# A selective scan on one core: 11 of every 32 readout multiplications moved from VectorE to GpSimd, and the accumulation on TensorE put one unit later

## The chip, the core and the metric

The kernel runs on one core of a Trainium2 chip. A core has five engines that run their own instruction queues in order and wait for each other through semaphores: TensorE (PE; its weight loads are PEld), VectorE (DVE), ScalarE (ACT), GpSimd (POOL) and SyncE (SP, which here only issues DMAs). SBUF and PSUM are the two on-chip memories; both have 128 partitions. The metric is the device time of one execution in microseconds, lower is better. The kernel before takes 8464.05 us, the median of five runs (8449.98 to 8479.84).

## The reference, cut to what matters

The whole computation is a two-layer network on an image batch of 2 x 128 x 64 x 64. Layer 0 is a deformable convolution block and a mixture of experts; layer 1 is a state-space block (a selective scan) and a second mixture of experts. The change touches only the scan of layer 1:

```
delta = softplus(delta + dt_proj_b)
A = -exp(A_log)
dA  = exp(delta * A)             # for each of 256 channels, 16 states n, 4096 positions l
dBu = delta * B[n, l] * x
s[l] = dA[l] * s[l-1] + dBu[l]
y[l] = sum over n of s[l, n] * C[n, l]
y = (y + x * D) * silu(z)
out = out_proj_w @ y
```

So for each channel, state and image there is a first-order recurrence over 4096 positions, and its states are multiplied with C and summed over the 16 states.

## The kernel before, in words

**Pieces and units.** The positions of an image are cut into 8 pieces of 512 (`LC`), so two images make 16 pieces. In a piece the 16 states and the 2 halves of the channels make 32 *units*; a unit is one tile of 128 channels x 512 positions. The loop of `scan` (from L1286 on) goes through all 512 units. The program keeps the order in which instructions are written (`manual_schedule`), so the order of every queue is the order of this loop.

**One unit u.** VectorE runs the recurrence as one scan instruction (L1301). It reads the decay `da` from PSUM and the input `db` from SBUF and writes the states back over `da` in PSUM. Then VectorE multiplies the states with C (`bc[:, 1, :]`), which gives `sc` in SBUF (L1311; the pool has 5 buffers of it). TensorE transposes the four 128-column blocks of `sc` with an identity and adds them up in a PSUM tile `py` (`add`, L1271); these additions stand at the end of the loop's body and take the `sc` of the unit before. ScalarE copies the last column of the states to `state` for the next piece (`keep`, L1308, one unit later).

**What is made ahead.** `drive` (L1246) lets GpSimd multiply `du` with B into `db`, three units ahead (`AHEAD`), with four buffers, so `db` of unit u+3 can only be written when the scan of unit u-1 is done. `decay` (L1253) lets ScalarE compute `da` two units ahead, in three PSUM buffers, so `da` of unit u+2 can only be written when unit u-1 has been read. `fetch` has SyncE broadcast rows of B and C (`bcb`).

**The side work.** While a piece is scanned, the next one is prepared by a generator (`prepare`), two steps a unit: 12 GpSimd multiplications and additions of 128x512 (L1151 x4, L1156 x2, L1166 x2, L1185 x2, L1213 x2), and on VectorE L1159 x2, L1195, L1197, L1204 x3, L1206 and L1209. `project` closes the piece before with three more (L1347 x2, L1362). While the first image is scanned, a second generator (`rest`) runs five steps a unit: the end of layer 0 and the convolutions of layer 1 for the second image, on TensorE, ScalarE, VectorE and by DMA.

Of the kernel before, what the change touches and what calls it, by code (L numbers as in the profile page):

```python
# [9 lines left out]
F32 = mybir.dt.float32  # L10
I32 = mybir.dt.int32
AF = mybir.ActivationFunctionType
ALU = mybir.AluOpType
# [5 lines left out]
P = 128  # L19
# [20 lines left out]
DS = 16  # L40
LC = 512
# [793 lines left out]
TB = 1  # L835
AHEAD = 3
BCB = 6


def view(ap, offset, dims):  # L840
# [28 lines left out]
class L1Conv:  # L869
# [351 lines left out]
    def scan(self, sp, ps, pp, rest):  # L1221


        env, nc = self.env, self.env.nc
        states = [sp.tile([P, 2, DS], F32, name=f"state{b}", bufs=1) for b in range(B)]
        for state in states:
            nc.vector.memset(state, 0.0)
        NK = N // LC

        def nxt(k):  # L1230

            res = {}
            return self.prepare(k // NK, k % NK, sp, pp, res), res

        gen, res = nxt(0)
        for _ in gen:
            pass
        units = [(k, n, half) for k in range(B * NK) for n in range(DS) for half in range(2)]
        pieces, das, dbs, bcb, tail = {0: res}, {}, {}, {}, iter(())

        def drive(u):

            if u < len(units):
                k, n, half = units[u]
                dbs[u] = sp.tile([P, LC], F32, name="db", bufs=AHEAD + 1)
                nc.gpsimd.tensor_tensor(dbs[u], pieces[k]["du"][:, half, :], bcb[u // 2][:, 0, :], ALU.mult)  # L1246

        def decay(u):
            if u < len(units):
                k, n, half = units[u]  # L1250
                das[u] = ps.tile([P, LC], F32, name="da", bufs=3)
                dl = pieces[k]["dl"][:, half, :]
                nc.scalar.activation(das[u], dl, AF.Exp, scale=self.A[:, half, n : n + 1])  # L1253

        def fetch(i):
            for i in range(len(bcb), i + 1):
                k, n = divmod(i, DS)
                if "bc" not in pieces.get(k, {}):
                    break
                bcb[i] = sp.tile([P, 2, LC], F32, name="bcb", bufs=BCB)  # L1260
                nc.sync.dma_start(out=bcb[i], in_=pieces[k]["bc"][n].partition_broadcast(P))

        adds, py = deque(), []

        def add(half, what, first, last):

            if first:
                py.append(ps.tile([P, GT, P], F32, name=f"py{half}", tag=f"py{half}", bufs=1))
            out = py[half]
            for j in range(GT):  # L1270
                nc.tensor.matmul(  # L1271
                    out[:, j, :],
                    what[:, j * P : (j + 1) * P],
                    env.ident,
                    is_transpose=True,
                    start=first and j == 0,
                    stop=last and j == GT - 1,
                )

        fetch(BCB - 3)  # L1280
        for u in range(AHEAD):
            drive(u)
        decay(0)
        decay(1)
        side, keep = Side(), None
        for u, (k, n, half) in enumerate(units):  # L1286
            now, i, state = pieces[k], u // 2, states[k // NK]
            if n == 0 and half == 0:
                side.add(tail)
            last = n == DS - 2 and half == 0  # L1290
            if last and k == NK - 1:
                rest.drain()

            if k + 1 < B * NK and k + 1 not in pieces and (k != NK - 1 or not rest.todo):
                gen, pieces[k + 1] = nxt(k + 1)
                side.add(gen)
            fetch(i + BCB - 2)
            bc = bcb[i]

            s = das.pop(u)  # L1300
            nc.vector.tensor_tensor_scan(s, s, dbs.pop(u), state[:, half, n : n + 1], ALU.mult, ALU.add)  # L1301
            if last:
                side.drain()
                fetch(i + BCB - 2)
            drive(u + AHEAD)

            if keep:
                nc.scalar.copy(*keep)  # L1308
            decay(u + 2)
            sc = sp.tile([P, LC], F32, name="sc", bufs=5)  # L1310
            nc.vector.tensor_tensor(sc, s, bc[:, 1, :], ALU.mult)  # L1311
            keep = state[:, half, n : n + 1], s[:, LC - 1 : LC]
            for _ in range(2 if rest.todo or k != NK - 1 else 4):
                side.step()
            for _ in range(5):
                rest.step()

            while adds:
                add(*adds.popleft())
            if n == 0 and half == 0:  # L1320
                py.clear()
                adds.extend((h, now["dx"][:, h, :], True, False) for h in range(2))
            adds.append((half, sc, False, n == DS - 1))
            if n == DS - 1 and half == 1:
                add(*adds.popleft())
                yt = sp.tile([P, 2, GT, P], F32, name="yt", bufs=1)
                tail = self.project(k // NK, k % NK, tuple(py), yt, now["zz"], now["xr"], pp)
        for _ in tail:
            pass
# [311 lines left out]
```

## Time and profile before

One execution was profiled. It took 8480.65 us, 0.8 us above the slowest of the five runs; its span from the first to the last instruction of the program is 8478.9 us, so 1.75 us lie outside.

| stretch of the span, us | length, us | what runs |
|---|---|---|
| 0 to 6101.7 | 6101.7 | layer 0, and layer 1's convolutions of the first image |
| 6101.7 to 7473.2 | 1371.5 | scan of the first image (units 0 to 255) beside the rest of the second image's earlier stages |
| 7473.2 to 8027.0 | 553.8 | scan of the second image, pieces 8 to 14 (units 256 to 479) |
| 8027.0 to 8093.8 | 66.8 | the last piece (units 480 to 511); nothing more is prepared |
| 8093.8 to 8478.9 | 385.1 | the second mixture of experts |

Over the span VectorE is busy 5712.4 us (67%), GpSimd 4588.7 us (54%), ScalarE 2127.9 us (25%) and TensorE 5962.2 us (70%). In the page's rows, `out<-in` names the tiles that an instruction writes and reads; then come the number of instructions, the busy time, the mean duration in ns and, after a bar, the idle time of the engine just ahead of these instructions with what ended it. In the list of waits, a line says who waited for whom, the sum in us, the number of times and the longest one. A bare number pair at the head of a timeline row is the start and the duration in us.

### The profile page before, as it was taken

The page shows a single profiled execution, that of the slowest core. Times are in us where ns is not written, and L with a number is a line of the kernel's source. Part 1 is how long each engine was busy: PE and PEld are TensorE (multiplying, and loading weights), DVE is VectorE, ACT ScalarE, POOL GpSimd, SP SyncE. Part 2 cuts the span into 40 slices and gives each one's busy share as a digit, 9 for nine tenths or more (in the row PEclk, how much of TensorE's full clock was granted, in tenths as well). Part 3 has the DMA queues.
Part 4 walks back from the last instruction along what each step waited for, and adds up shares of the span by engine and source line. Part 5 has one row for each costly group of instructions (what it writes and reads, how often), then busy time and mean ns, then how long its engine had stood idle before and what let it go on. Part 6 is the DMA issues. An engine that isn't in the chain of part 4 may idle for free. (4 is left out here: it accounts for less than half of the span.)

```text
span 8478.9 us, 85143 instructions
## 1 busy us (share of the span) xinstructions
PE 5962.2 (70%) x28533; PEld 4203.4 (50%) x28533; DVE 5712.4 (67%) x8472; ACT 2127.9 (25%) x4442; POOL 4588.7 (54%) x4556
## 2 busy tenths in 40 slices
PE   2678888888888857667666676667556566755569
PEld 2456666666666635344434343444344455533359
DVE  1577777777777767777886658666557735599940
ACT  1111111111111114111112121212353444555520
POOL 0456666666666666665665656666534323367600
PEclk7789999999989979878888878888766655656555
DMA  4677666666666678777777777776553334334323
GB/s 125 183 245 216 196 206 213 194 214 193 208 212 194 213 221 274 250 227 220 222 233 201 218 210 223 216 214 199 168 178 112 114 89 121 110 120 136 126 89 124
DMA packets 658558, 1574.35 MB, mean 186 GB/s; under 512 B 168164, under 2 KB 280588, under 8 KB 645580
## 3 DMA queue, kind: packets, MB, share of 16 engines
q0 software_dynamic: 307200, 1006.88, 39.8%
q1 hardware_dynamic: 287980, 494.19, 18.5%
q10 hardware_dynamic: 62944, 67.83, 2.3%
q8 instruction: 232, 3.80, 0.2%
q14 instruction: 202, 1.65, 0.1%
HBM read 1450.99 MB, written 120.01 MB: 185 GB/s over the span
## 5 line engine op out<-in xcount | busy, mean ns | idle before, releaser
L547 POOL DMA_INDIRECT v<-table,idx x3840 | 3649.7, 950 | 2394.8 <-issue 995.4
L597 PE MATMUL out<-st,regw 128*128 128x512 f32 x3840 | 2120.0, 677 | 164.5 <-issue 110.0
L558 DVE TENSOR_TENSOR v<-v,pw 128x1024 f32<-128x1024 f32 x960 | 1168.8, 1218 | 1075.4 <-DMA v<-table,idx 917.1
L568 PE MATMUL pst<-ident,v 128*128 128x128 f32 x7680 | 1243.5, 305 | 800.1 <-issue 482.6
L577 ACT COPY st<-pst 128x512 f32<-128x512 f32 x960 | 558.6, 586 | 4345.9 <-remote 2485.3
L568 PEld LDWEIGHTS pst<-ident,v 128*128 128x128 f32 x7680 | 1008.0, 157 | 1142.5 <-issue 755.5
L564 DVE TENSOR_TENSOR v<-v,low 128x512 f32<-128x512 f32 x1920 | 1318.2, 687 | 65.6
L563 DVE TENSOR_TENSOR low<-v,pw 128x512 f32<-128x512 f32 x1920 | 1329.3, 692 | 33.4
L1246 POOL TENSOR_TENSOR db<-du,bcb 128x512 f32<-128x512 f32 x512 | 660.6, 1295 | 956.6 <-DVE da L1301 909.5
L597 PEld LDWEIGHTS out<-st,regw 128*128 128x128 f32 x3840 | 763.3, 221 | 770.6 <-issue 707.6
L334 PEld LDWEIGHTS po<-wout,ring 128*128 128x128 f32 x5120 | 743.2, 199 | 369.5 <-issue 367.7
L334 PE MATMUL po<-wout,ring 128*128 128x147 f32 x5120 | 798.7, 300 | 162.8 <-issue 158.0
L1301 DVE TENSOR_TENSOR_SCAN da<-da,state,db 128x512 f32<-128x512 f32 x512 | 657.1, 1283 | 292.9 <-ACT da L1253 274.6
L1271 PE MATMUL py<-ident,sc 128*128 128x128 f32 x2048 | 466.8, 381 | 333.6 <-DVE sc L1311 333.0
L1271 PEld LDWEIGHTS py<-ident,sc 128*128 128x128 f32 x2048 | 341.9, 198 | 475.6 <-DVE sc L1311 436.5
L1311 DVE TENSOR_TENSOR sc<-da,bcb 128x512 f32<-128x512 f32 x512 | 354.1, 692 | 48.6 <-DVE da L1301 1.9
L1253 ACT ACTIVATE da<-delta,w_A_log 128x512 f32<-128x512 f32 x512 | 354.0, 692 | 17.3 <-DVE delta L1209 1.5
L972 PE MATMUL ps<-tm,X 120*88 120x48 f32 x2048 | 254.9, 304 | 75.8 <-ACT Y L924 36.7
L972 PEld LDWEIGHTS ps<-tm,X 120*88 120x88 f32 x2048 | 250.3, 219 | 107.9 <-ACT Y L924 49.3
L959 PE MATMUL ps<-ident,hs 64*120 64x64 f32 x1408 | 142.8, 271 | 136.5 <-ACT X L924 87.9
L959 PEld LDWEIGHTS ps<-ident,hs 64*120 64x120 f32 x1408 | 125.7, 177 | 197.6 <-ACT X L924 105.6
L988 PE MATMUL ps<-ident,Y 88*64 88x88 f32 x768 | 109.1, 294 | 144.7 <-ACT img L924 86.6
(268 smaller groups left out, 5090.8 us busy)
## 6 DMA issues: line engine op xcount, KB each, us to landing
bcb<-bc SPq DMA_DIRECT2D x256, 512.0 KB
regw<-in_regw SPq DMA_DIRECT2D x66, 1280.0 KB
v<-table,idx POOLq DMA_INDIRECT x3840
yd<-ys ACTq DMA_DIRECT2D x128, 256.0 KB
yc<-yd SPq DMA_DIRECT2D x32, 1024.0 KB
gb<-gd SPq DMA_DIRECT2D x16, 2048.0 KB
tm<-pos SPq DMA_DIRECT2D x16, 1440.0 KB
table<-xn SPq DMA_DIRECT2D x128, 128.0 KB
```

The source lines that it names most:

```text
L334: m()
L547: nc.gpsimd.indirect_dma_start(out=v[:, j, :], out_offset=None, in_=self.table[b], in_offset=bass.IndirectOffsetOnAxis(ap=idx[:, j, t : t ...
L558: nc.vector.tensor_tensor(up, up, w, ALU.mult)
L563: nc.vector.tensor_tensor(low, v4[:, two, 2:4, :], w, ALU.mult)
L564: nc.vector.tensor_tensor(up[:, two], up[:, two], low, ALU.add)
L568: nc.tensor.matmul(pt[:, j, :], v4[:, j, q, :], env.ident, is_transpose=True, start=j == 0 and q == 0, stop=j == GT - 1 and q == 1,)
L577: nc.scalar.copy(st, pt.rearrange("p j t -> p (j t)"))
L597: nc.tensor.matmul(self.out[half], self.regw[t // CH][:, t % CH, half * P : (half + 1) * P], st, start=first, stop=last,)
L972: nc.tensor.matmul(ps[:, c, :], X[:, c0 + c, :], tm[:, :, c0 + c], start=True, stop=True)
L1246: nc.gpsimd.tensor_tensor(dbs[u], pieces[k]["du"][:, half, :], bcb[u // 2][:, 0, :], ALU.mult)
L1271: nc.tensor.matmul(out[:, j, :], what[:, j * P : (j + 1) * P], env.ident, is_transpose=True, start=first and j == 0, stop=last and j == GT ...
L1301: nc.vector.tensor_tensor_scan(s, s, dbs.pop(u), state[:, half, n : n + 1], ALU.mult, ALU.add)
```

## The change

In units 2, 5, 7, 10, 13, 15, 18, 21, 23, 26 and 28 of each piece the scan writes its states to the `sc` tile in SBUF instead of over `da` in PSUM, and the multiplication with C is done by GpSimd, in place, in the unit after, behind that unit's `db` on GpSimd's queue. In the other 21 units nothing moves on VectorE. For all units, the additions on TensorE come two units behind instead of one; what is left is added at the end of the piece. No buffer is added. In the changed kernel `db` is written at L1247, the scan stands at L1305, the new GpSimd multiplication at L1316 and the one left on VectorE at L1321.

```diff
+ASIDE = (2, 5, 7, 10, 13, 15, 18, 21, 23, 26, 28)
...
-        side, keep = Side(), None
+        side, keep, lag = Side(), None, None
...
             s = das.pop(u)
-            nc.vector.tensor_tensor_scan(s, s, dbs.pop(u), state[:, half, n : n + 1], ALU.mult, ALU.add)
+            aside = u % (2 * DS) in ASIDE
+            sc = sp.tile([P, LC], F32, name="sc", bufs=5)
+            to = sc if aside else s
+            nc.vector.tensor_tensor_scan(to, s, dbs.pop(u), state[:, half, n : n + 1], ALU.mult, ALU.add)
...
             decay(u + 2)
-            sc = sp.tile([P, LC], F32, name="sc", bufs=5)
-            nc.vector.tensor_tensor(sc, s, bc[:, 1, :], ALU.mult)
-            keep = state[:, half, n : n + 1], s[:, LC - 1 : LC]
+
+            if lag:
+                nc.gpsimd.tensor_tensor(*lag, ALU.mult)
+                lag = None
+            if aside:
+                lag = sc, sc, bc[:, 1, :]
+            else:
+                nc.vector.tensor_tensor(sc, s, bc[:, 1, :], ALU.mult)
+            keep = state[:, half, n : n + 1], to[:, LC - 1 : LC]
...
-            while adds:
-                add(*adds.popleft())
+            while adds and adds[0][0] <= u:
+                add(*adds.popleft()[1:])
             if n == 0 and half == 0:
                 py.clear()
-                adds.extend((h, now["dx"][:, h, :], True, False) for h in range(2))
-            adds.append((half, sc, False, n == DS - 1))
+                adds.extend((u + 2, h, now["dx"][:, h, :], True, False) for h in range(2))
+            adds.append((u + 2, half, sc, False, n == DS - 1))
             if n == DS - 1 and half == 1:
-                add(*adds.popleft())
+                while adds:
+                    add(*adds.popleft()[1:])
```

## The prediction

> **What bounds the kernel now.** I cut the span where the scan's first, 257th, 481st and last unit start, and read the engines' busy time by stretch.
>
> ```profile
> core 0: us, PE busy (x) PEld busy (x) DVE busy (x) ACT busy (x) POOL busy (x), PEclk, DMA share, GB/s
> 0.00:6101.70 6101.70, 4455.28 (x21169) 3016.80 (x21169) 4242.27 (x6531) 1082.50 (x2365) 3666.81 (x3858) 0.85 0.69 211
> 6101.70:7473.20 1371.50, 851.86 (x4556) 669.44 (x4556) 813.07 (x1098) 661.37 (x1332) 495.52 (x364) 0.63 0.40 120
> 7473.20:8027.00 553.80, 295.13 (x1176) 194.42 (x1176) 526.47 (x533) 316.57 (x609) 390.12 (x309) 0.60 0.39 131
> 8027.00:8093.80 66.80, 40.48 (x165) 29.74 (x166) 62.35 (x68) 27.43 (x65) 36.22 (x29) 0.55 0.26 91
> ```
>
> The second row is the first image's scan (stretch A), the third pieces 8 to 14 (B), the fourth the last piece (C). In B and C VectorE is 95% and 93% busy: it is the bound, at 553.8 / 7 = 79.1 us a piece; GpSimd is 70% busy. In A VectorE is 59% busy and no engine is full. The rest of the span isn't touched.
>
> Next the groups of B by shape: four of VectorE's, then GpSimd's largest, from two answers of one view.
>
> ```profile
> L1301 DVE TENSOR_TENSOR_SCAN da<-da,state,db 128x512 f32<-128x512 f32 x224 | 287.2, 1282 | 0.0
> L1311 DVE TENSOR_TENSOR sc<-da,bcb 128x512 f32<-128x512 f32 x225 | 155.6, 692 | 21.4 <-DVE da L1301 0.9
> L1159 DVE SCALAR_TENSOR_TENSOR xs<-xc,w,xs 128x512 f32<-128x512 f32 x14 | 21.1, 1545 | 0.0
> L1195 DVE TENSOR_SCALAR q<-e 128x1024 f32<-128x1024 f32 x7 | 10.1, 1446 | 4.8 <-ACT state L1308 4.8
> ...
> L1246 POOL TENSOR_TENSOR db<-du,bcb 128x512 f32<-128x512 f32 x225 | 287.8, 1285 | 143.5 <-DVE da L1301 137.7 <-POOL db L1246 4.7 <-issue 1.1
> ```
>
> A multiplication costs VectorE 0.69 us and GpSimd 1.28. GpSimd's idle 143.5 us are waits for the scan that frees a `db` buffer, so it has room now. Last, VectorE's timeline at unit 21 of a piece, then GpSimd's.
>
> ```profile
> 7677.74 1.28 DVE L1301 TENSOR_TENSOR_SCAN da<-da,state,db 128x512 f32<-128x512 f32 x1
> 7679.13 0.69 DVE L1311 TENSOR_TENSOR sc<-da,bcb 128x512 f32<-128x512 f32 x1
> 7679.74 2.29 DVE L1195 TENSOR_SCALAR q<-e 128x1024 f32<-128x1024 f32 x1
> ...
> 7676.52 4.96 POOL L1246 TENSOR_TENSOR db<-du,bcb 128x512 f32<-128x512 f32 x4
> ```
>
> From scan to next operation 7677.74 to 7679.74 = 2.00 us, of which 0.61 from `sc` on. L1195 needs 0.69 us alone (its minimum) and took 2.29: it ended 0.55 us after GpSimd's four back-to-back multiplications did (7681.48). So some VectorE operations stand still while GpSimd works, and the change gives GpSimd more work.
>
> **The change, part by part.** The instruction order of the built kernel shows what it says: 16 x 11 = 176 multiplications leave VectorE and 176 (M) join GpSimd, each right behind a `db` (D); ScalarE, SyncE and the DMAs keep their counts.
>
> *VectorE.* A moved `sc` frees its 0.61 us, and 0.04 to 0.17 more, as the next operation no longer has to wait for the scan's result: I take 0.70, so 7.7 us a piece. A scan from PSUM into SBUF isn't in the trace. `sc` has those places, at 0.69, and the 676 ns of L1362 next to it differ by 0.02 us; 0.02 x 176 = 3.5 us bounds it either way, and I take 0.
>
> *GpSimd in B.* A piece has 32 D, 12 operations for the next piece and now 11 M. Back to back they start 4.96 / 4 = 1.24 us apart: 55 x 1.24 = 68 us, under VectorE's 79.1 - 7.7 = 71.4. But the work is uneven. From the D written in unit 6 to the one that unit 21's scan needs (written in unit 18) GpSimd has 13 D, 5 M and 9 others: 27 x 1.24 = 33.5, and 0.9 where L1159 holds it up (two GpSimd operations of 1.71 instead of 1.27): 34.4 us. The scan of unit 5 lets this begin (four `db` buffers), and VectorE's own way from unit 21 to the next piece's unit 5, read from the timeline with 0.71 off for each of the six moved `sc` among them, is 42.2 us. Together 76.7 us a piece: GpSimd becomes the bound between units 6 and 20, and 2.4 of the 7.7 us are left. In that path L1195 stands with 2.29 us. GpSimd now comes to it with more queued work, so I add one more operation's wait, 1.24: **78.0 us**, 1.1 less a piece, 8 us in seven. The ends: 71.4 (all VectorE's saving, -54 us) and, if L1195 waits for all seven GpSimd operations then ready (7 x 1.24 - 1.3 + 0.55 = 7.9 instead of 2.29; the 1.3 is the scan ahead of it), 76.7 + 5.6 = 82.3, +22 us.
>
> The Trainium skill ("SBUF — State Buffer", section "SBUF: two separate sides") says that VectorE operations with two SBUF inputs or in a 2-port mode and GpSimd operations exclude each other for a whole instruction, whoever starts first. L1159's pattern agrees; L1195 lost a turn (2.29, where one GpSimd operation would make it about 0.69 + 1.27 = 1.96). By the rule the piece would be 76.4 and the whole change some 11 us better than my sum. "Perfetto Trace Analysis", section "Optimizing Scalar/DVE Operations", speaks against the change: because of this port, moving work between the two might not help. But `sc` took 690 to 694 ns in all 225 cases of B beside a busy GpSimd, so the moved operation itself didn't suffer from it, nor should the scan, with one SBUF input.
>
> *New waits.* M waits for ScalarE's `state` copy of the same unit, since it overwrites what that reads. Behind M stand the preparation's operations and the D three units ahead, and the scan waits for them. The copy's own wait is for `sc` (159.0 us in B, 119 times); in a moved unit it has the scan alone to wait for, and D stands ahead of M, 1.27 us: hidden; without that cover 1 us for each of 11, inside the ends above. The scan itself now waits for an `sc` buffer, last read by the additions of five units before, which come one unit later. In B they start with `sc`'s end and have two units, 4 us, to spare: 0.
>
> *C.* No preparation: 43 x 1.24 = 53.3 us for GpSimd against 63.4 - 7.7 = 55.7. VectorE stays the bound: **-7 us**.
>
> *A.* 88 `sc` move, at most 88 x 0.7 = 62 us. The waits of A:
>
> ```profile
> DVE da L1301 <- ACT da L1253: 274.6, 65, 21.4
> ACT state L1308 <- DVE sc L1311: 147.8, 53, 16.0
> ...
> PE py L1271 <- DVE sc L1311: 80.3, 43, 7.5
> ```
>
> VectorE often waits itself, so most `sc` are hidden. I followed the releasers back from the scan that opens B: 84 of 256 `sc` lie on this chain, 33 of them in moved units, with 20.4 us. Another path takes over soon; I take **-15** with what TensorE's waits for `sc` give by the later addition. Against it: in about 15% of A's units the scan five units on starts before TensorE has ended the next unit's additions, so about 13 moved scans would wait 1 to 3 us. TensorE is the late one there, so I take 0, and +25 for the end.
>
> **Sum.** -8 - 7 - 15 = -30: 8480.65 - 30 = 8450.7 by the profiled execution. That stands 16.6 above the median of 8464.05, so I forecast 8434. Less than 0.2%, 17 us, can't be told from no change.
>
> **Rivals.**
> 1. *GpSimd's burst costs nothing*, because it is far enough ahead when the preparation starts. Then B gives -54, C -7 and A -20 to -62: 8341 to 8383. For it: GpSimd's 143.5 us idle in B. Against it: the 27 operations counted above.
> 2. *No change.* GpSimd is the bound to unit 21 and A's chain finds another path: B and A 0, C -7: 8457, within 17 us of before.
> 3. *Slower.* The port, in one place: at units 21 to 23 GpSimd arrives with its backlog, L1195 waits for all of it (82.3), and L1197 and L1204 behind it lose a turn of 1.24 each (84.8). B then costs +22 to +40; with C, and nothing from A, 8479 to 8497; I take 8493. For it: the 2.29 us row. Against it: L1195 waited so long in three of seven pieces, and L1159, with the same conflict, got its turn after one operation. It makes B even when L1195 takes 4.7 us, and the kernel slower by 0.2% from 8.1.
>
> **Chances and range.** Forecast 47% (own range 8414 to 8447), rival 1 15%, rival 2 22%, rival 3 16%. Faster by over 0.2%: 62%, same 22%, slower 16%. The range 8385 to 8485 leaves out most of rival 1 and half of rival 3, and takes in A's and B's nearer ends.
>
> **What would show it.** In the changed profile: `sc` on VectorE x336, M x176 at about 1.27; pieces of B 76 to 79 us, with GpSimd over 85% busy and scans that wait for `db` around units 13 to 21; L1195's mean over 2.3; C 7 us shorter; A 0 to 30 us shorter, with fewer PE waits for `sc`. It is wrong if the scan into SBUF takes over 1.30, if M or D stretch beyond 1.4, if scans wait for `py`, or if B comes to 72 or to 82 us a piece.

## The result, and the profile after

The changed kernel takes **8483.55 us** (median of 30 runs, 8464.44 to 8505.57); the kernel before, run beside it, took 8457.13 us (55 runs). The ratio is 1.0027, with a 95% interval of 1.0021 to 1.0033: slower by 18 to 28 us, where I had forecast 30 us less. The time lies at the upper end of my range, on the side to which I had given 16%.

The profiled execution of the changed kernel has a span of 8461.9 us. It was one of the short ones: its first stretch, which the change doesn't touch, was 6085.8 us instead of 6101.7. So spans are not compared here, but stretches, cut at the same units as in the prediction. The engines' busy time by stretch (length, then PE, PEld, DVE, ACT, POOL; the rows are A, B and C):

```profile
core 0: us, PE busy (x) PEld busy (x) DVE busy (x) ACT busy (x) POOL busy (x), PEclk, DMA share, GB/s
6085.80:7459.10 1373.30, 846.94 (x4555) 670.25 (x4555) 769.57 (x1010) 649.34 (x1332) 623.76 (x451) 0.64 0.41 120
7459.10:8026.10 567.00, 279.32 (x1177) 202.48 (x1176) 506.79 (x457) 309.00 (x609) 498.38 (x385) 0.61 0.38 128
8026.10:8083.50 57.40, 33.36 (x168) 28.02 (x167) 54.45 (x57) 26.76 (x65) 49.51 (x41) 0.65 0.34 107
```

In every stretch VectorE has less to do, as intended: 43.5 us less in A (813.07 to 769.57), 19.7 in B, 7.9 in C. Only C became shorter. In B VectorE fell from 95% to 89% busy and the stretch grew by 13.2 us; in A 43.5 us of work became 45.3 us more idle time. From the first scan of piece 15 to its last one (the measure that I use for C from here on) C went from 63.6 to 54.3 us.

| stretch | forecast | profile, after minus before | one part alone, against before on its chip |
|---|---|---|---|
| A | -15 | +1.8 | aside_first: ratio 1.0015 (1.0006 to 1.0024), +5 to +18 us |
| B | -8 | +13.2 | aside_second (B and C together): 1.001 (0.9998 to 1.0021), -2 to +16 us |
| C | -7 | -9.3 | in aside_second |
| sum | -30 | +5.7 | the whole, 1.0027: +18 to +28 us |

The two parts measured alone give 0.0015 + 0.001 = 0.0025, which is the whole within its interval. The profile's three differences add up to less. But the profiled lengths of A scatter: aside_second and later_adds (experiments 2 and 3) run the same program in A and have 1349.7 and 1340.8 us, the changed kernel has 1373.3 and, on another chip, 1353.5. So for A the ratio in the last column is the better number. For the second part that ratio alone doesn't exclude no change.

The groups of B by shape, from the same two answers of one view as before (VectorE's, then GpSimd's; count, busy us, mean ns, idle time ahead of them):

```profile
L1305 DVE TENSOR_TENSOR_SCAN da<-da,state,db 128x512 f32<-128x512 f32 x148 | 189.4, 1280 | 12.4 <-ACT state L1312 8.9 <-POOL db L1247 1.9 <-ACT da L1254 0.9
L1321 DVE TENSOR_TENSOR sc<-da,bcb 128x512 f32<-128x512 f32 x148 | 102.3, 691 | 16.0 <-PE py L1272 3.3
L1305 DVE TENSOR_TENSOR_SCAN sc<-da,state,db 128x512 f32<-128x512 f32 x77 | 98.1, 1274 | 9.1 <-PE py L1272 9.1
...
L1196 DVE TENSOR_SCALAR q<-e 128x1024 f32<-128x1024 f32 x7 | 34.4, 4921 | 3.3 <-ACT state L1312 2.8 <-ACT e L1194 0.5
L1160 DVE SCALAR_TENSOR_TENSOR xs<-xc,w,xs 128x512 f32<-128x512 f32 x14 | 21.8, 1557 | 16.7 <-POOL xs L1152 16.7
...
L1247 POOL TENSOR_TENSOR db<-du,bcb 128x512 f32<-128x512 f32 x224 | 295.2, 1328 | 52.1 <-DVE da L1305 26.5 <-DVE sc L1305 24.7 <-PE py L1272 0.9
L1316 POOL TENSOR_TENSOR sc<-sc,bcb 128x512 f32<-128x512 f32 x77 | 108.5, 1409 | 1.3 <-ACT state L1312 1.3
```

The reader is to see three things. What moved suffers little: a scan into SBUF takes 1274 ns and one into PSUM 1280, `sc` on VectorE is at 691 ns as before, and only GpSimd's multiplication `sc` has a mean of 1409. GpSimd's idle time ahead of `db` fell from 143.5 to 52.1 us. And one instruction a piece, L1196 (L1195 before), went from a mean of 1446 ns to 4921, which is 24.3 us in seven pieces. Beside it stand waits that before had none of: 16.7 us of L1160 for GpSimd's L1152, 12.4 us (9.1 and 3.3) of scans and `sc` for TensorE's additions `py`, 8.9 us of scans for ScalarE.

The timeline at unit 21 of piece 10, VectorE's rows and then GpSimd's (start and duration in us):

```profile
7669.65 1.28 DVE L1305 TENSOR_TENSOR_SCAN sc<-da,state,db 128x512 f32<-128x512 f32 x1 [0.83 <-PE py L1272]
7671.41 6.90 DVE L1196 TENSOR_SCALAR q<-e 128x1024 f32<-128x1024 f32 x1 [0.47 <-ACT state L1312]
7678.34 1.22 DVE L1198 TENSOR_TENSOR q<-q,e 128x1024 f32<-128x1024 f32 x1
...
7670.35 1.27 POOL L1247 TENSOR_TENSOR db<-du,bcb 128x512 f32<-128x512 f32 x1
7671.58 1.27 POOL L1316 TENSOR_TENSOR sc<-sc,bcb 128x512 f32<-128x512 f32 x1
7672.81 3.73 POOL L1247 TENSOR_TENSOR db<-du,bcb 128x512 f32<-128x512 f32 x3
7676.49 1.26 POOL L1316 TENSOR_TENSOR sc<-sc,bcb 128x512 f32<-128x512 f32 x1
```

L1196 asks at 7671.41, while GpSimd is in the multiplication of 7670.35. Five more follow it back to back, and L1196 ends at 7678.31, 0.56 us after the last of them (7677.75). It stood still until GpSimd's queue ran dry. In the next piece, and in this one alone of the seven, the same meeting went the other way:

```profile
7753.12 0.77 DVE L1196 TENSOR_SCALAR q<-e 128x1024 f32<-128x1024 f32 x1 [0.47 <-ACT state L1312]
...
7752.06 1.27 POOL L1247 TENSOR_TENSOR db<-du,bcb 128x512 f32<-128x512 f32 x1
7753.29 1.72 POOL L1316 TENSOR_TENSOR sc<-sc,bcb 128x512 f32<-128x512 f32 x1
```

The start of L1196 stands to GpSimd's operations as in the piece of 6.90 us, within 0.02 us (it starts 1.06 us after the one and 0.17 us ahead of the other, both times), but now it ends 0.56 us after the one operation in progress, and the next one of GpSimd is stretched, to 1.72. That piece took 77.1 us; the four pieces with 6.9 us took 82.1, 81.7, 81.9 and 82.0. If L1196 had always got its turn so early, B would be some 7 x 77.1 = 540 us: an estimate from one piece, which no run shows by itself (see state_pool in experiment 7).

### The profile page after: what moved, and what is told of

Read it like the earlier page. It is cut to its first block, busy times and chain, and to the rows that moved or that the text cites. A ratio compares the mean times of both kernels' runs of the same rounds, so it can differ in the third digit from the quotient of the medians.

```text
span 8461.9 us, 85172 instructions
## 1 busy us (share of the span) xinstructions
PE 5922.2 (70%) x28533; PEld 4204.1 (50%) x28533; DVE 5641.2 (67%) x8296; ACT 2107.9 (25%) x4442; POOL 4839.3 (57%) x4732
## 5 line engine op out<-in xcount | busy, mean ns | idle before, releaser
L597 PE MATMUL out<-st,regw 128*128 128x512 f32 x3840 | 2120.7, 677 | 133.3 <-issue 79.3
L1247 POOL TENSOR_TENSOR db<-du,bcb 128x512 f32<-128x512 f32 x512 | 677.6, 1334 | 325.9 <-DVE sc L1305 159.4
L1272 PE MATMUL py<-ident,sc 128*128 128x128 f32 x2048 | 447.6, 384 | 366.8 <-POOL sc L1316 308.1
L1272 PEld LDWEIGHTS py<-ident,sc 128*128 128x128 f32 x2048 | 362.8, 204 | 470.6 <-POOL sc L1316 341.8
L1305 DVE TENSOR_TENSOR_SCAN da<-da,state,db 128x512 f32<-128x512 f32 x336 | 430.3, 1281 | 191.8 <-ACT da L1254 165.0
L1316 POOL TENSOR_TENSOR sc<-sc,bcb 128x512 f32<-128x512 f32 x176 | 242.4, 1377 | 454.8 <-ACT state L1312 453.7
L1305 DVE TENSOR_TENSOR_SCAN sc<-da,state,db 128x512 f32<-128x512 f32 x176 | 224.3, 1274 | 132.9 <-PE py L1272 73.7
L1321 DVE TENSOR_TENSOR sc<-da,bcb 128x512 f32<-128x512 f32 x336 | 232.3, 691 | 102.3 <-PE py L1272 73.8
L973 PE MATMUL ps<-tm,X 120*88 120x48 f32 x2048 | 257.5, 305 | 54.7 <-DMA tm<-pos 20.6
```

What stands on the lines that cost most here:

```text
L597: nc.tensor.matmul(self.out[half], self.regw[t // CH][:, t % CH, half * P : (half + 1) * P], st, start=first, stop=last,)
L973: nc.tensor.matmul(ps[:, c, :], X[:, c0 + c, :], tm[:, :, c0 + c], start=True, stop=True)
L1272: nc.tensor.matmul(out[:, j, :], what[:, j * P : (j + 1) * P], env.ident, is_transpose=True, start=first and j == 0, stop=last and j == GT ...
L1305: nc.vector.tensor_tensor_scan(to, s, dbs.pop(u), state[:, half, n : n + 1], ALU.mult, ALU.add)
```

## The experiments

The ratios are each against the kernel before on the same chip. These were other chips than that of the first result, with times of before of 7646.47 us (fold_after, fold_before, later_adds, aside_second), 7653.51 (moved_aside, aside_first, after_again, stt_const), 7648.72 (state_pool, moved_psum, before_psum, moved_all) and 8380.99 (first_pool, moved_psum_pool, after_psum); the untouched first stretch differs between chips, the scan's pieces hardly. Every kernel here computes the whole function.

**My theory after the result:** in B, VectorE's instructions that read two tiles from SBUF, and L1196, share something with GpSimd and stand still until its queue is empty (the *port*); GpSimd comes to unit 21 with a long queue, because twelve operations of the preparation and the moved multiplications (M) stand together in units 6 to 20. **The rivals:** GpSimd is simply late, and whatever VectorE does next pays for it (the *backlog* alone); or GpSimd simply has too much work in B, wherever it stands (the *load*); or the loss comes from the additions, which now stand two units behind.

**1. The polynomial without its L1196** (fold_after; fold_before is the same edit in the kernel before). The factor goes into the last square, and one instruction goes.

```diff
+SQUARES[-1] = tuple(v * (-LINEAR[0]) ** (1.0 if i == 2 else 0.5) for i, v in enumerate(SQUARES[-1]))
...
-        nc.vector.tensor_scalar(q, e, LINEAR[0], LINEAR[1], ALU.mult, ALU.add)
...
-        nc.vector.tensor_tensor(q, q, e, ALU.mult)
...
+        nc.vector.scalar_tensor_tensor(q, e, LINEAR[1] / LINEAR[0], e, ALU.add, ALU.mult)
...
-        nc.vector.scalar_tensor_tensor(dl, v, 0.0, q, ALU.max, ALU.add)
+        nc.vector.scalar_tensor_tensor(dl, v, 0.0, q, ALU.max, ALU.subtract)
```

> The changed kernel without L1195: (a*e + b)*e is folded into one scalar_tensor_tensor (e + b/a)*e, the factor goes into the last square and the sign into the last subtraction. Port theory (B, the stretch of pieces 8 to 14, loses only because L1195 stands still while GpSimd works off its backlog; 34.4 us of it in B, against 10.1 before): B falls from 567 to about 536 to 542 us, with no new waits of scans for db over 5 us in all. Backlog theory (GpSimd's work between units 6 and 20 is the bound and L1195 only shows it): scans wait for db instead, B stays at 558 to 567.

> The kernel before with the same folding. Both theories: B loses L1195's 10.1 us and little else, 553.8 to about 543 us; the first image's scan (A) 0 to 6 us shorter; the kernel 10 to 17 us faster than before. The difference to the changed kernel with the same folding is the worth of the change without the port's wait: by the port theory this one is 0 to 8 us the slower in B and 9 us the slower in the last piece, by the backlog theory 15 us or more the faster in B.

fold_after: 1.0007 (0.9996 to 1.0019), B 557.9 us. fold_before: 0.9988 (0.9979 to 0.9998), B 550.3. B is 9.1 us shorter than the changed kernel's 567.0, with an instruction less, but still 7.6 above fold_before's: the fold doesn't cure the stall, its one instruction takes the place of the one removed. VectorE's group in fold_after's B:

```profile
L1198 DVE SCALAR_TENSOR_TENSOR q<-e 128x1024 f32<-128x1024 f32 x7 | 34.7, 4954 | 3.4 <-ACT state L1312 3.4
```

Its mean is 4954 ns; single ones took up to 7.80 us. So it isn't the form of L1196 that matters, and the 536 to 542 us that I had expected if it did are missed. What follows: the next instruction that meets GpSimd's burst stands still in the same way. The piece in which it took only 1.31 us is again the shortest, 75.5 us; the other six took 79.8 to 81.1.

**2. The additions two units behind, and nothing moved** (later_adds).

```diff
-ASIDE = (2, 5, 7, 10, 13, 15, 18, 21, 23, 26, 28)
+ASIDE = ()
```

> Only the additions two units behind; no multiplication moves (ASIDE is empty). Port theory: within 5 us of the kernel before in all, B 553 to 555 us. Ring theory (the sc buffers have one unit less of slack, and A loses the 17 us that the profiles of the two kernels do not show): 12 to 20 us slower, in A, with more waits of VectorE for py than the 5 us of before.

0.9996 (0.9987 to 1.0006), B 555.3, C 63.3: no effect that can be measured. The rival of the additions falls, as a cause by itself.

**3. The halves of the change** (aside_second: multiplications moved in the second image's pieces alone; aside_first, with `k < NK` in the place of `k >= NK`: in the first image's alone).

```diff
-            aside = u % (2 * DS) in ASIDE
+            aside = k >= NK and u % (2 * DS) in ASIDE
```

> Multiplications move only in the second image's 8 pieces; additions two units behind everywhere. Port theory: B 567 us and the last piece 54 us as in the changed kernel, A as before: 4 us slower than before in all. If A's moved multiplications cost the rest of the 26 us between the medians, this kernel is about 20 us faster than the changed one; if not, it is as slow as that.

> Multiplications move only in the first image's 8 pieces. Burst theory: B and the last piece as with the later additions alone (555 and 63 us), A within 8 us of before, the kernel within 8 us of before. If the moved multiplications of A cost what the stretches of one profile do not show: 12 to 20 us slower, in A.

aside_second: 1.001 (0.9998 to 1.0021), B 571.9, C 54.7. aside_first: 1.0015 (1.0006 to 1.0024), A 1357.9, with B at 555.9. The first half costs beyond its interval. For the second the interval takes in no change; its profile has B 18.1 us longer and C 8.9 shorter. That A may cost as much as B and C together was news to me: no rival of the prediction had its loss in A.

**4. The same number of moved units, but none in units 8 to 21** (moved_aside).

```diff
-ASIDE = (2, 5, 7, 10, 13, 15, 18, 21, 23, 26, 28)
+ASIDE = (1, 3, 5, 7, 22, 23, 24, 25, 26, 28, 30)
```

> The changed kernel with the same number of moved multiplications, 11 a piece, but in units 1, 3, 5, 7, 22 to 26, 28 and 30, away from the 12 operations that prepare the next piece. Burst theory (GpSimd's queue between units 8 and 21 is the cause, by the port and by what waits for the preparation): B falls to 500 to 515 us, L1196 back to 0.7 to 2.3 us, the last piece 54 to 58 us; 40 to 60 us faster than the kernel before in all. Load theory (GpSimd at 88% of B is too much wherever it stands, as GpSimd and VectorE shut each other out): B 545 to 567 us.

0.9986 (0.9977 to 0.9995), B 552.4, C 59.0. L1196 is cured: 1.19 us in six pieces, 1.91 in one. But B is far from the 500 to 515 us that the burst alone would have given back, and within the 545 to 567 of the load. The timeline at unit 12, VectorE's rows and GpSimd's:

```profile
6809.43 8.47 DVE L1160 SCALAR_TENSOR_TENSOR xs<-xc,w,xs 128x512 f32<-128x512 f32 x2
6817.82 1.28 DVE L1305 TENSOR_TENSOR_SCAN da<-da,state,db 128x512 f32<-128x512 f32 x1
...
6810.55 1.25 POOL L1152 TENSOR_TENSOR xs<-xs,tap 128x512 f32<-128x512 f32 x1
6811.77 1.25 POOL L1157 TENSOR_TENSOR zc<-zc,sab 128x512 f32<-128x512 f32 x1
6812.99 1.25 POOL L1247 TENSOR_TENSOR db<-du,bcb 128x512 f32<-128x512 f32 x1
6814.21 1.25 POOL L1157 TENSOR_TENSOR zc<-zc,sab 128x512 f32<-128x512 f32 x1
6815.43 1.25 POOL L1247 TENSOR_TENSOR db<-du,bcb 128x512 f32<-128x512 f32 x1
```

The stall has gone to L1160, two taps of the causal convolution that read two tiles from SBUF. Of the pair's 8.47 us the first has 7.81: it ends at 6817.24, 0.56 us after GpSimd's last operation (6816.68), and the second, with GpSimd idle, takes 0.74. GpSimd is here not late at all: behind 6816.68 it waits 2.49 us for a scan. That speaks for the port and against the backlog alone. In six of the seven pieces the first tap takes 7.5 to 7.8 us and the piece 79.3; in the one where it takes 1.21, the piece takes 76.6.

**5. L1196 with a second input** (stt_const), a broadcast constant column instead of the constant; and the changed kernel once more on that chip (after_again).

```diff
+        self.lin = wp.tile([P, 2], F32, name="lin")
+        nc.vector.memset(self.lin, LINEAR[1])
...
-        nc.vector.tensor_scalar(q, e, LINEAR[0], LINEAR[1], ALU.mult, ALU.add)
+        nc.vector.scalar_tensor_tensor(q, e, LINEAR[0], self.lin.unsqueeze(2).to_broadcast([P, 2, LC]), ALU.mult, ALU.add)
```

> The changed kernel with L1196 as a scalar_tensor_tensor whose second input is a broadcast column in SBUF, 1.2 us alone instead of 0.7: two SBUF inputs instead of a 2-port mode. If only the 2-port mode loses its turn to a GpSimd that works back to back, L1196 takes 1.2 to 2.5 us and B falls by 15 to 25 us; if any instruction that needs the shared port does, it takes up to 7.4 us and B stays at 565 to 575.

> The changed kernel once more, for a second profile and for its time on this chip beside the others. By its first profile, B +13 and the last piece -9 against before, A the same: 4 us slower. By its first timing: 0.27%, 20 to 26 us slower.

stt_const: 7676.85 us in its only run, B 574.8, and the instruction's mean is 5952 ns: the form with one streamed input was not the trouble. after_again: 1.0035 (1.0023 to 1.0047), B 571.4, C 54.3; the result repeats.

**6. One input from PSUM** (moved_psum: the places of 4, and the last tap made by ScalarE in PSUM; before_psum: the same tap in the kernel before; after_psum: the tap, with the changed kernel's own places). The addition that is left on VectorE then has one input in SBUF.

```diff
+            t3 = bank([P, LC], "t3")
+            nc.scalar.mul(t3, xc[:, h, 3 : 3 + LC], w1(h, 3))
...
-            nc.vector.scalar_tensor_tensor(u, xc[:, h, 3 : 3 + LC], w1(h, 3), u, ALU.mult, ALU.add)
+            nc.vector.tensor_tensor(u, t3, u, ALU.add)
```

> The moved placement (units 1, 3, 5, 7, 22 to 26, 28, 30), and VectorE's operation at unit 12 (L1160, 10.3 us a piece in that unit, where it lost its turn to GpSimd) gets its tap from ScalarE in PSUM, so that it has one SBUF input and needs no shared port. Port theory: unit 12 falls to 3 to 6 us, B from 552 to 515 to 530 us, the kernel 30 to 45 us faster than before. Load theory (GpSimd at 88% has to be waited for anyway): scans or the next port operation wait instead and B stays at 545 to 553.

> The kernel before with the same tap in PSUM. Unit 12 falls from 4.9 to 3.2 us, as nothing waits for the port there: B 541 to 545, the kernel 8 to 15 us faster than before. Both theories say so; it is the measure for what the moved placement is worth beyond it.

> The changed kernel with its own units, and only the last tap of the causal convolution taken through PSUM, so that L1160 no longer has two SBUF inputs. Port theory: L1160 no longer loses a turn (about 1 us, twice a piece) but the preparation and the moved multiplications still stand together ahead of unit 21, so the polynomial's first operation waits through the queue there as before: 79 to 81.5 us a piece, 1.000 to 1.003 of before. Rival: the place of the moved units does not matter and L1160 was the whole trouble: 75.5 to 76.5 us a piece and 0.995 to 0.997.

moved_psum: **0.9956 (0.9944 to 0.9967)**, the fastest kernel of the study, with B at 529.6 us and every piece at 75.6 or 75.7. before_psum: 0.9991 (0.998 to 1.0003), B 551.7, where I had expected 541 to 545. So the tap is worth little by itself; what it does is to let the moved multiplications pay. The load is excluded as what cost moved_aside its gain: GpSimd does the same operations here, and B is 22.8 us shorter. moved_psum's B, by stretch row and two of VectorE's groups (the line numbers are 2 higher than in the changed kernel):

```profile
6638.80:7168.50 529.70, 275.21 (x1176) 193.19 (x1176) 465.29 (x457) 317.96 (x623) 505.96 (x386) 0.60 0.40 137
```

```profile
L1198 DVE TENSOR_SCALAR q<-e 128x1024 f32<-128x1024 f32 x7 | 10.4, 1483 | 4.7 <-ACT state L1314 2.3 <-ACT e L1196 2.3
...
L1162 DVE TENSOR_TENSOR xs<-t,xs 128x512 f32<-128x512 f32 x14 | 9.7, 690 | 11.7 <-POOL xs L1152 11.7
```

The tap takes 690 ns all 14 times, beside the same burst that held L1160 for a mean of 3852 ns in moved_aside. With the input its kind has changed too, to a `tensor_tensor`; but L1198 of the changed kernel, a `tensor_tensor` with both inputs in SBUF, was held as well, up to 2.17 us where it needs 1.22, so the kind alone doesn't protect. GpSimd is now 95.5% busy in B (505.96 of 529.7), so there is little left to move to it: from here on the load is close to being the limit.

after_psum: 1.0007 (0.9998 to 1.0016), B 567.9:

```profile
L1198 DVE TENSOR_SCALAR q<-e 128x1024 f32<-128x1024 f32 x7 | 39.9, 5695 | 4.3 <-ACT state L1314 4.3
...
L1162 DVE TENSOR_TENSOR xs<-t,xs 128x512 f32<-128x512 f32 x14 | 9.6, 686 | 18.2 <-POOL xs L1152 18.2
```

With the changed kernel's places the tap is cured too (686 ns) but now waits longer for its input from GpSimd (18.2 us), and the polynomial's first operation stands 5.7 us a piece. So both are needed, the place and the port: a burst ahead of unit 21 costs B its gain, whatever L1160 does. (The whole stands at 1.0007, nearer to before than the changed kernel's 1.0027; B doesn't show where that comes from.)

**7. GpSimd copies the state itself** (state_pool: the changed kernel; first_pool: aside_first; moved_psum_pool: moved_psum; moved_all: moved_psum_pool with the fold of 1). M overwrites what ScalarE's copy of the last column reads, so it waits for that copy; here the copy stands ahead of M on GpSimd's own queue.

```diff
-                nc.scalar.copy(*keep)
+                (nc.gpsimd.tensor_copy if lag else nc.scalar.copy)(*keep)
```

> The changed kernel, but in the moved units GpSimd itself copies the last state, ahead of its multiplication, so that GpSimd no longer waits for ScalarE's copy (437 to 452 us of waits in A). If that wait is what A's moved multiplications cost (the kernel with them in the first image alone was 0.15% slower): A 8 to 15 us shorter, the kernel 8 to 15 us faster than the changed one, so 12 to 18 us slower than before; B unchanged within 5 us. If A's cost is TensorE's wait for GpSimd or the sc buffers: as slow as the changed kernel, 24 to 27 us over before.

> Multiplications move only in the first image's pieces, with the later additions, and GpSimd itself copies the last column of the states in the moved units. Without that copy the same kernel took 1.0015 of before. Theory: what the move costs in the first image's scan is GpSimd's queue standing behind the wait for ScalarE's copy; with it gone the change gains there, 0.9965 to 0.9998 of before, and the waits for ScalarE's state copy ahead of the moved multiplications (452 us in that stretch) are gone. Rival: the first image's loss comes from the additions that come later or from TensorE waiting for a multiplication twice as long, and the gain of the copy on GpSimd was made in the second image's scan: still 1.001 to 1.0025.

> The moved places (units 1, 3, 5, 7, 22 to 26, 28, 30), the last tap through PSUM, and the state copies of the moved units on GpSimd. If the two losses are separate (port in the second image's scan, wait for ScalarE's copy in the first one's) the gains add: moved_psum stood at 0.9956, so 0.991 to 0.9945, and pieces of 75 to 76 us as in moved_psum. Rival: 11 copies of about 0.34 us a piece fall on GpSimd where it is late, so the pieces go to 77 to 79.5 us and the whole to 0.995 to 0.998.

> Moved placement, tap in PSUM, states copied by GpSimd in moved units, and L1196 folded into the next operation. Port theory: B 505 to 525 us, last piece 55 to 59, 35 to 60 us faster than before. Load theory: B 540 to 553, not over 15 us faster than before.

state_pool: 0.9987 (0.9979 to 0.9996), where the changed kernel stood at 1.0027 and 1.0035; B 559.7, C 54.3. That is better than my expectation for it (12 to 18 us slower than before), and in a place where I expected nothing: B is 7.3 and 11.7 us shorter than in the two profiles of the changed kernel. first_pool: 1.0004 (0.9994 to 1.0014), where aside_first stood at 1.0015. moved_psum_pool: 0.9978 (0.9966 to 0.9989), B 549.5. moved_all: 0.9974 (0.9965 to 0.9984), B 543.9; I had expected 505 to 525 for its B by the port, 540 to 553 by the load.

In B of state_pool L1196 no longer stands still, though the moved units are those of the changed kernel:

```profile
L1196 DVE TENSOR_SCALAR q<-e 128x1024 f32<-128x1024 f32 x7 | 7.4, 1053 | 3.3 <-ACT state L1312 3.3
```

It took 1.03 to 1.07 us in all seven pieces, and yet B is 559.7 us and not 540. The copies are 25.9 us of GpSimd's time in B, and GpSimd is busy for 526.4 us of it, 94%. So the stall of L1196 is not all that keeps B long: without it GpSimd's load is near the limit, here with the copies on top. Why L1196 gets its turn here stays open.

In A the longest wait of the changed kernel is this one (who waited for whom: us in total, times, longest):

```profile
POOL sc L1316 <- ACT state L1312: 452.5, 58, 28.2
DVE da L1305 <- ACT da L1254: 164.1, 49, 16.2
...
PE py L1272 <- POOL sc L1316: 71.5, 20, 8.8
DVE sc L1321 <- PE py L1272: 70.5, 16, 11.6
DVE sc L1305 <- PE py L1272: 64.7, 12, 14.2
```

In first_pool its first line is gone, and the others are not:

```profile
POOL db L1247 <- DVE da L1305: 325.0, 75, 16.1
POOL db L1247 <- DVE sc L1305: 272.5, 48, 22.2
DVE da L1305 <- ACT da L1254: 152.9, 48, 15.4
...
PE py L1272 <- POOL sc L1316: 72.6, 19, 10.1
DVE sc L1321 <- PE py L1272: 70.3, 17, 10.8
DVE sc L1305 <- PE py L1272: 58.8, 12, 14.2
```

GpSimd's waits are now for the scans, as they were before the change (750.8 us ahead of `db` then). Between kernels with and without GpSimd's copy, on different chips, A's profiled length went from 1357.9 (aside_first) to 1342.6, and from 1353.5 (after_again) to 1343.1 (state_pool): 10 to 15 us, about the size of A's loss. That would make M's wait for the copy what the change lost in A, but the scatter of A is as large as this, and the ratios 1.0015 and 1.0004 have intervals that overlap. And moved_aside speaks against it. It keeps ScalarE's copy and waits long for it in A:

```profile
POOL sc L1316 <- ACT state L1312: 336.8, 54, 28.0
```

Yet its A took 1331.0 us, where aside_first and after_again on the same chip took 1357.9 and 1353.5. A part of the loss can be placed: the seventh piece of A took 142.9 to 147.0 us in the five kernels that move nothing in A, 148.8 to 153.8 in the six with the changed kernel's units and ScalarE's copy, still 148.3 and 148.2 with GpSimd's copy (state_pool, first_pool), and 144.0 in moved_aside. So the choice of the units matters in A as well, the copy is at most a part, and the cause of A's loss is not shown. L1196's stall isn't it: in that piece it took 0.9 us in the changed kernel. What the copy doesn't bring is the gain that I had forecast for A; first_pool stands at no change, and my expectation for it (a gain) missed.

In moved_psum_pool the copies cost:

```profile
L1314 POOL COPY state<-sc 128x1 f32<-128x1 f32 x77 | 28.9, 376 | 0.0
```

11 a piece at 376 ns are 4.1 us on an engine that was 95.5% busy; the piece went from 75.6 to 78.5 us. The two remedies don't add: where GpSimd has no room left, as in B of moved_psum, its copies cost. A version with the copies on GpSimd in A alone wasn't tried.

## Why the prediction was wrong, by its steps

**VectorE's saving, and the scan into SBUF: right.** I took 0.70 us a moved unit; the undisturbed units went from 1.98 to 2.00 us down to 1.19, so 0.79. I took 0 for the scan into SBUF, and 1274 ns against 1280 confirms it.

**C: right in kind.** -7 forecast, 63.6 to 54.3 = -9.3 measured; 11 x 0.79 = 8.7 accounts for it. Here nothing is prepared, GpSimd has no burst, and the change does all that it can.

**B: the first step that failed** is "GpSimd now comes to it with more queued work, so I add one more operation's wait, 1.24: 78.0 us". L1196 was priced at 2.29 + 1.24 = 3.53 us; its mean was 4.92, as 6.90 in four pieces, 3.05 in two and 0.77 in one. I had both prices written down: the far end, 7.9 us and 82.3 a piece, was rival 3's, and with 6.90 the pieces came to 81.7 to 82.1. The one piece in which it won took 77.1. So the sum was sound (34.4 and 42.2 are 76.6, not 76.7, which changes nothing) and the choice within it wrong: between "one more turn" and "the whole queue" I took the first since L1195 had waited only in three pieces of seven before, and since L1159 got its turn after one operation. But a longer queue makes each lost turn longer, and the row of 2.29 already showed an instruction that ended 0.55 us after GpSimd's *last* multiplication: it had waited for a queue of two to run dry, not for a turn. Read that way, the row gave the right price.

In the path's two legs: from the end of unit 5's scan to unit 21's start I had 34.4 us, and the trace has 35.1 to 35.5 in five pieces, 37.4 in two. From there to the next unit 5's end I had 42.2 + 1.24 = 43.4, and it is 46.6 in the four pieces with 6.90, 43.7 in the two with 3.05, 42.0 in the one with 0.77. GpSimd did become the bound in units 6 to 20, as I wrote: its 27 operations there took 34.1 to 34.9 us, and it is 87.9% busy in B. But the sign that I gave for it, scans that wait for `db`, hardly came: 1.9 us in B. VectorE met GpSimd's lateness at L1196, and through the `sc` buffer and L1160, which follow. Of my signs of being wrong three came: scans wait for `py`, M has a mean of 1.409 us in B, and pieces come to 82 us.

**The `sc` buffer: priced 0, wrong.** I wrote that the additions "start with `sc`'s end and have two units, 4 us, to spare". In the changed kernel an addition of a moved unit starts with M's end, and M stands in GpSimd's backlog. The waits of B:

```profile
PE py L1272 <- POOL sc L1316: 216.8, 56, 7.2
...
DVE xs L1160 <- POOL xs L1152: 16.7, 7, 2.4
DVE sc L1305 <- PE py L1272: 9.1, 7, 2.5
```

TensorE waits 216.8 us for M in B, and passes some of it on to the scans: 12.4 us with the 3.3 of `sc`. In piece 12, where L1196 took 3.04 us, the scan of unit 21 waited 2.45 us for `py` and an `sc` just before it 1.10; this piece and the next, with 3.05, took 81.1 us too. So the backlog has two ways to the path, the port and the buffer, and a piece that escapes the one may meet the other.

**L1160.** Its wait for GpSimd's L1152, 2.4 us a piece, was in no term of mine. I had counted L1152 among the 27 operations of GpSimd, but not that VectorE itself reads its result at unit 12, before unit 21.

**M's wait for ScalarE's copy.** In B it was 1.3 us, so "hidden" was right there. In A I priced it by the same sentence, and it was 452.5 us on GpSimd's queue. There ScalarE also has the second image's stages, and waits itself for TensorE (109.7 us for `ps` alone); I looked at the copy's waits in B alone. What this wait cost the kernel is not shown (experiment 7).

**A: -15 forecast, +5 to +18 measured (aside_first).** This is the second step that failed: I took 20.4 us of moved `sc` on one chain as time that A would lose in part, and 0 for the new waits. VectorE's busy time did fall by 43.5 us, but its waits mostly changed their names: those of the scans for ScalarE's `da` went from 274.6 to 164.1 and 53.1 (the scans that write `sc`), and those of `sc` and of the scans for `py` from 0 to 135.2 (70.5 + 64.7). later_adds, which moves nothing, has 69.4 of these for `py` already and is no slower as a whole. I had named this wait with 0 and +25 as its ends and took 0. What the net loss in A comes from stays open (experiment 7): the seventh piece shows a part of it, and neither the wait for ScalarE's copy nor the later additions explain it by themselves.

**The rivals.** Rival 3 gave 8479 to 8497, and the time is 8483.55, but not wholly by its way: B cost +13 in the profile (up to +18 in after_again, 571.4 against 553.8), less than its +22 to +40. L1198 and L1205 behind L1196 didn't lose 1.24 us each: their means are 1632 and 1668 ns, where before they were 1225 and 1559. A's loss, for which it had nothing, filled the place: that the total falls into its range is partly luck. Rival 1 is excluded by the pieces of 82 us, though moved_psum shows what it would need: its B, 529.6 us, is a good part of the way to the 500 us that it gave.

**The rule of the skill.** The Trainium skill ("SBUF — State Buffer", section "SBUF: two separate sides") has the two engines exclude each other for a whole instruction, whoever starts first. The trace agrees that each holds the other up (L1196 6.90; a GpSimd operation stretched to 1.72 behind L1196's 0.77). It disagrees with the turn that I read into the rule: five operations that GpSimd started after L1196 went ahead of it. The sentence of "Perfetto Trace Analysis", section "Optimizing Scalar/DVE Operations", that moving work between these two might not help, was the right warning: VectorE's moved scans were unharmed (1274 ns), and operations left behind paid.

## What to carry to other kernels

Before moving work to GpSimd, list the VectorE instructions that stay and read two tiles from SBUF, and look at what GpSimd has queued when each of them starts: price such an instruction at the whole back-to-back queue, not at one turn. Then place the moved work where none of them follows, and take one of their inputs from PSUM where that can't be had; here only both together turned +0.27% into -0.44%. And read the busy share in short stretches: an engine at 88% over a piece had a run of 27 operations almost without a gap in it (at most 0.8 us in all), and its consumers are reached through every buffer that it holds, not only the one on the path.

## What the runs showed of the hardware that I had not expected

- **Who wins between VectorE and GpSimd is not given by the order of arrival that the trace shows.** With starts alike within 0.02 us, L1196 took 6.90, 6.89, 6.90 and 6.90 us in four pieces and 0.77 in one. What decides it stays open.
- **It isn't a matter of the instruction's form.** The one-input operation with constants (4.9 us mean), the same with a broadcast column (6.0) and the fold with two streamed inputs (5.0) stand alike; an addition with one input in PSUM took 690 ns at the place where the tap with two inputs in SBUF took 3.9 us.
- **The chip matters for the total, and not for the scan.** The first stretch took 6.10 ms on the first chip, 5.28 to 5.30 on three others and 6.01 to 6.03 on the last; a piece of B with the kernel's VectorE work as before took about 79 us on all of them.
